# v of the graph convolutions in seven half-block products, its neighbours moved along the LSTM's places

## The chip, the cores and the metric

The kernel runs on one core of a Trainium2 chip. The metric is the device time of one execution in microseconds (us), lower is better; the median of the runs is given. All data are float32. The engines are called PE (TensorE, matrix products), DVE (VectorE), ACT (ScalarE), POOL (GpSimd) and SP (SyncE, which here only issues DMAs).

## The reference

Four residual layers with a layer norm and a relu ahead of each work on x of 128 x 64 x 256 (batch, tokens T, channels D). Layer 0 is a normalised aggregation with a two-layer MLP and batch norms, layers 2 and 3 are attention with one and four heads. The change lies in layer 1:

```python
h = jax.nn.relu(jnp.einsum('ts,bsh->bth', adj, x @ Wg0 + bg0))
h = jax.nn.relu(jnp.einsum('ts,bsh->bth', adj, h @ Wg1 + bg1))
for p in range(1, MAX_SKIP + 1):
    wins = h[:, :nw * p, :].reshape(Bv * nw, p, Hd)
    last = _lstm_last(Wih[p - 1], Whh[p - 1], bih[p - 1], bhh[p - 1], wins)
    h = h.at[:, idx, :].set(last.reshape(Bv, nw, Hd))
```

Two graph convolutions are followed by LSTMs over windows of 1, 2, 3 and 4 tokens, each of which reads what the one before has written to h.

## The kernel before

**Tiles and order.** The batch is cut into 16 chunks of 512 rows (8 batch entries of 64 tokens); two chunks make a superchunk (SUP = 2), so there are 8. The LSTM of layer 1 works on one superchunk at a time: `lstms` (L1443) yields for the windows p = 1 (`single`), 2, 3, 4 (`lstm`, from L1073). While superchunk sc is in its LSTM, the kernel issues between the LSTM's segments the graph convolutions of the chunks of superchunk sc+1, the residual and next layer's norms of the superchunks before, and the first steps (scaling, a reload in another order) of the chunks of sc+2. I call one pass of this loop a round; seven rounds (sc 0 to 6) contain convolutions, and the first of the eight superchunks gets its own ahead of the loop (`first_convolutions`, which the change leaves alone).

The order is written out by hand: PE, DVE, ACT, POOL and SP are under a manual schedule, so that each engine executes in the order in which the program issues. The loop at L1602 counts the segments. Each `yield` of an LSTM makes the next whole number n, a `yield "a"` a half more; these numbers are the *places*, 0 to 21 in a round:

```python
for mark in lstms(sc, hTs[sc]):
    n = n + 0.5 if mark else int(n) + 1
    for u in todo.pop(n, ()):
        next(u)
```

`todo` comes from tables (L1559 to 1570): `CONV[i]` lists for chunk i of a superchunk (0 is called even, 1 odd here) the places at which the steps of `convolutions` are taken, `BEGUN[i]` the places of its first steps, one round ahead; `FIRST` stands for `CONV` in round 0. Window 2 covers places 4 to 7, window 3 places 8 to 13, window 4 places 14 to 21. A place at the end of a window (7, 13) lies between the last cell of one LSTM and the first products of the next.

**The convolution of a chunk** (`convolutions`, L999) has these steps: scaling with layer 0's batch norm (`scaled`, DVE); transposes of 32 x 32 blocks on DVE and a write to DRAM (`put`); its reading back in another order (`get`); `add_squares` onto x (DVE, L298); two halves of layer norm statistics (DVE, L195); two halves of their application (ACT); aggregation over the graph (PE, agg_b, two banks of PSUM); its copies to SBUF (DVE, L1025); `product_v`, v = agg @ Wg0, as 8 PE passes with 512 columns (L934); `bounded` (DVE, L940), which takes the maximum with the negated bias, that is a relu with the bias shifted into a later constant; `product_u`, u = v @ Wg1, 16 PE passes with 256 columns (L948); `biased` (DVE, L954), which adds the constant c2; the second aggregation (agg_c); and two steps of relus to hT (ACT, L959), from which the LSTM reads.

**The LSTM.** Each gate product is made from seven products of half blocks (L1133 for the first step, L1186 for later ones), whose operands' differences POOL or DVE makes (`differences`, L323) and whose parts DVE adds (L1140, L1195) and ACT copies (L1137, L1192). A step ends with a cell on DVE (L1265, L1266), a tanh on ACT (L1267) and the new state on DVE (L1110 to l_hs inside a window; L1112 and L1116 to hT in its last step; k=0 and k=1 are the two halves of the channels). PSUM has four tags with two banks each: x, y, z for the LSTM and ps for the convolutions. Tag x holds product 6 and then product 7 of the same gate in the same half bank; between the two the DVE addition of product 6 has to read it.

Of the kernel before, what the change touches and what calls it, by code (L numbers as in the profile page):

```python
# [8 lines left out]
F32 = mybir.dt.float32  # L9
AF = mybir.ActivationFunctionType  # L10
OP = mybir.AluOpType
AX = mybir.AxisListType

P = 128
# [5 lines left out]
def kernel(  # L20
# [22 lines left out]
    nc = tc.nc  # L43
    B, T, D = x.shape
    H0 = w1t.shape[1]
    KD = D // P
# [653 lines left out]
    with tc.manual_schedule(engines={mybir.EngineType.PE}):  # L700
# [5 lines left out]
        wqkv_sb = stage.tile([P, KD, 3 * D], F32, name="wqkv_sb")  # L706
        wo_sb = stage.tile([P, KD, D], F32, name="wo_sb")
        bg0_sb = stage.tile([P, D], F32, name="bg0_sb")
        bg1_sb = const.tile([P, D], F32, name="bg1_sb")
        wg1_st = stage.tile([P, KD, D], F32, name="wg1_st")  # L710
        nc.sync.dma_start(wqkv_sb, wqkv.rearrange("(k p) f -> p k f", p=P))
        nc.sync.dma_start(wo_sb, wo.rearrange("(k p) f -> p k f", p=P))
        nc.sync.dma_start(bg0_sb, bg0.partition_broadcast(P))
        nc.sync.dma_start(bg1_sb, bg1.partition_broadcast(P))
        nc.sync.dma_start(wg1_st, wg1.rearrange("(k p) f -> p k f", p=P))

        wt = stage.tile([P, 3 * KD, D], F32, name="wt")
# [153 lines left out]
    bias2 = const.tile([P, SKIP, KG], F32, name="bias2")  # L871
    nc.sync.dma_start(bias, bih)
    nc.sync.dma_start(bias2, bhh)

    wih1 = [lasting.tile([P, 3, n, P], F32, tag=f"wih1_{n}", name=f"wih1_{n}") for n in (4, 3)]

# [50 lines left out]
    def by_batch(agg):  # L927
        return agg.rearrange("p k (j e t) -> p e (k j) t", e=2, t=T)
# [12 lines left out]
                                    banks[m].rearrange("p (j n) -> p j n", n=P),  # L941
                                    nc1[:, m, None, :].to_broadcast([P, NJ, P]), OP.max)

    def product_u(c, v):
        banks = [bank(f"u1_{c}_{t}").rearrange("p (j d) -> p j d", d=D) for t in range(NJ // 2)]
        for j in range(NJ):
            for k in range(KD):
                nc.tensor.matmul(banks[j // 2][:, j % 2, :], v[:, k, j * P : (j + 1) * P],  # L948
                                 wg1_sb[:, k, :], start=(k == 0), stop=(k == KD - 1))
        return banks  # L950

    def biased(u, banks):
        for t, ps in enumerate(banks):
# [45 lines left out]
    def convolutions(c):  # L999

        y, h = conv_tile(c)
        for m in range(KD):
            scaled(y, c, m)
        yield
        mid = res.tile([P, Q, CH * KD // Q], F32, tag=f"r{c}", name=f"ym_{c}")
        for k in range(KD):
            nc.vector.transpose(
                mid.rearrange("p b (j k c) -> p k j b c", j=NJ, k=KD)[:, k],
                y[:, k, :].rearrange("p (j b t) -> p j b t", b=Q, t=32))
        far = put(mid, f"y{c}")  # L1010
        yield
        dst = y.rearrange("p k (q n) -> p (k q) n", q=2)
        get(dst, far)
        xs[c] = res.tile([P, NJ, D], F32, tag=f"r{c}", name=f"xs_{c}")
        nc.sync.dma_start(xs[c], xr[c])
        yield
        add_squares(xs[c], xs[c], dst)
        yield
        for stats in norm_halves(xs[c], f"b{c}"):
            yield  # L1020
        yield from apply_halves(h, xs[c], stats, f"b{c}")
        banks = aggregate(h, adjt_bd, f"b{c}")
        yield
        for e, ps in enumerate(banks):
            nc.vector.tensor_copy(by_batch(y)[:, e], ps)  # L1025
        yield
        banks = product_v(c, y)
        yield
        bounded(y, banks)
        yield  # L1030
        banks = product_u(c, y)
        yield
        biased(h, banks)
        yield
        banks = aggregate(h, adjt_bd, f"c{c}")
        yield
        for e, ps in enumerate(banks):
            to_hT(c, e, ps)
            yield
# [518 lines left out]

    EARLY = 0, 3, 5, 7, 9, 9, 13, 15  # L1559
    RESIDUAL = (0, 6, 9), (5.5, 7, 9.5)  # L1560
    CONV = (3, 4, 5, 5.5, 7, 8, 9, 10, 10), (5, 5, 6, 9.5, 11, 11.5, 13, 14, 15, 15.5, 17, 18, 20)
    BEGUN = (11, 11.5, 12, 14.5, 17, 17, 20, 21), (17.5, 19, 19.5, 21)
    RESIDUAL_LAST = (0, 4, 5.5), (3, 5, 9)
    FIRST = (0.5, 0.5, 1, 3, 3, 4, 4, 5, 5.5, 7, 8, 9, 10, 10), (2, 3, 4, 5, 5, 5.5, 6, 9.5, 11, 11.5, 13, 14, 15, 15.5, 17, 18, 20)
    AHEAD = (9, 10), (10, 11)
    LATE = (4.5, 4.5, 5.5, 9, 19.5), (9.5, 9.5, 11, 12, 21)
    LATEST = (4.5, 4.5, 5.5, 9, 9.5), (9.5, 9.5, 10, 11, 11.5)
# [5 lines left out]
    with tc.manual_schedule(engines={mybir.EngineType.PE, mybir.EngineType.DVE, mybir.EngineType.Pool,  # L1573
                                     mybir.EngineType.SP}):
        new_hT(0)
        early = l1.tile([P, 4, KD, CH], F32, tag="gates", name="early", bufs=1)
        convs = {c: (convolutions if c >= SUP else first_convolutions)(c) for c in range(NCH)}
        aheads = {c: ahead(c) for c in range(NCH - SUP)}
        for n, i in enumerate(START):
            if n == 5:  # L1580
                nc.vector.tensor_add(c2, c2_ps[:, :D], bg1_sb)
                nc.vector.tensor_add(bias, bias, bias2)
            for at, fill, name in ((6, 16, "d"), (9, 6, "e"), (10, 6, "f")):
                if n == at:
                    keep_busy(fill, name)
            next(convs[i])
            if n == 1:
                nc.sync.dma_start(wg0_sb, wg0.rearrange("(k p) f -> p k f", p=P))
                nc.sync.dma_start(wg1_sb, wg1.rearrange("(k p) f -> p k f", p=P))
                singles = load_single()  # L1590
                next(singles)
                load_sets(6)
            if n == 9:
                next(singles)
    banks_of("psum1", x=2, y=2, z=2, ps=2)
# [736 lines left out]
```

## Time and profile before

| | |
|---|---|
| median of 2 runs | 1841.06 us (1840.62 and 1841.5) |
| the profiled execution | 1841.82 us |
| its span in the profile | 1839.9 us |
| granted TensorE clock | 0.999 |
| DVE, ACT and POOL busy | 1353.8, 1061.4 and 656.8 us |
| v of a chunk (L934, 8 passes) | 3.43 us on PE |
| u of a chunk (L948, 16 passes) | 3.45 us on PE |
| one round | about 152 us |

Busy time is what an engine's instructions cover; the share of the span is an average over all stages. A timeline line has the start and the duration in us, engine, line and operation, output<-input, shape, and the count of instructions put together; in square brackets the idle time ahead of it and what released it. Matmuls are pipelined, so that durations of neighbouring groups overlap, and what PE really spends is read from start to start.

A round as these places stood in it before (even chunk / odd chunk): agg_b at 3 / 11, its copies at 4 / 11.5, v at 5 / 13, bounded at 5.5 / 14, u at 7 / 15, biased at 8 / 15.5, agg_c at 9 / 17, relus at 10, 10 / 18, 20. For the chunks after these: scaling at 11 / 17.5, put at 11.5 / 19, get at 12 / 19.5, add_squares at 14.5 / 21.

### The profile page before, as it was taken

To read this page: it belongs to the slowest core of one execution; us is meant where nothing else is said; L and a number is where in the kernel's file an instruction comes from. 1 tells how busy PE (TensorE), PEld (TensorE's weight loads), DVE (VectorE), ACT (ScalarE), POOL (GpSimd) and SP (SyncE) were. 2 spreads that over 40 slices of the span, in tenths; PEclk is the share of its full clock that TensorE was granted. 3 is DMA by queue.
4 is the path that set the end of the run, shared out by engine and by line. 5 is a ranking of instruction groups with operands and counts; after the bars stand their busy time and mean duration, and the time that the engine had idled before them with its cause. 6 is when DMAs were issued, how large, how long until landed. Compare 5 with 4: busy or idle time off the path is not lost.

```text
span 1839.9 us, 41662 instructions
## 1 busy us (share of the span) xinstructions
PE 1813.3 (99%) x15847; PEld 1531.8 (83%) x15847; DVE 1353.8 (74%) x3475; ACT 1061.4 (58%) x2538; POOL 656.8 (36%) x916
## 2 busy tenths in 40 slices
PE   8999999999999999999999999999999999999998
PEld 6876866997897899699699789879968887898886
DVE  5768857577667777777777777776676677888897
ACT  5766636557457466655655746566565654455553
POOL 5865823223223321422321332232232215444542
PEclk9999999999999999999999999999999999999999
DMA  3213651233443342253443434225154146544534
GB/s 117 70 58 139 222 218 53 81 115 127 134 143 127 112 153 78 98 146 116 149 149 127 149 115 162 101 93 150 48 172 149 64 110 195 162 139 139 162 108 147
DMA packets 113415, 234.54 MB, mean 127 GB/s; under 512 B 11712, under 2 KB 77120, under 8 KB 113216
## 3 DMA queue, kind: packets, MB, share of 16 engines
q1 hardware_dynamic: 112320, 230.02, 38.5%
q8 instruction: 125, 2.05, 0.5%
q0 software_dynamic: 320, 1.05, 0.2%
q10 hardware_dynamic: 576, 0.82, 0.1%
q14 instruction: 74, 0.61, 0.1%
HBM read 164.21 MB, written 67.63 MB: 126 GB/s over the span
## 4 chain that ended last, share of the span: by engine, by line
PE 89%; DVE 5%; ACT 2%; POOL 2%; issue 1%; DMA 0%; SPq 0%; DVEq 0%; ACTq 0%; POOLq 0%
PE x L1186 23%; PE z L1186 11%; PE y L1186 6%; PE y L1133 4%; PE x L1368 4%; PE y L1368 3%; PE u L948 3%; PE v L934 3%; PE x L1133 3%; PE X L1938 3%; PE X L436 2%; PE X L512 2%; PE v L2062 2%; PE z L1133 2%; PE Y L1938 1%; PE X L1773 1%
## 5 line engine op out<-in xcount | busy, mean ns | idle before, releaser
L1101 ACT ACTIVATE l_gates<-l_gates,bias 128x256 f32<-128x256 f32 (+4 forms) x528 | 238.2, 498 | 210.9 <-DVE l_gates L1195 109.7
L1186 PE MATMUL x<-xd,wset 128*128 128x128 f32 (+2 forms) x1152 | 255.0, 303 | 0.8 <-ACT l_gates L1192 0.8
L1186 PE MATMUL x<-l_hd,wset 128*128 128x128 f32 (+2 forms) x1152 | 254.6, 303 | 0.0
L1252 POOL TENSOR_TENSOR l_gates<-l_gates 128x512 f32<-128x512 f32 (+2 forms) x48 | 75.3, 1570 | 368.0 <-ACT l_gates L1101 368.0
L1195 DVE TENSOR_TENSOR l_gates<-l_gates,x 128x128 f32<-128x128 f32 (+2 forms) x384 | 121.2, 321 | 97.8 <-PE x L1186 95.1
L1186 PEld LDWEIGHTS x<-xd,wset 128*128 128x128 f32 x1152 | 187.7, 191 | 6.4 <-issue 1.4
L1186 PEld LDWEIGHTS x<-l_hd,wset 128*128 128x128 f32 x1152 | 187.8, 191 | 5.0
L1195 DVE TENSOR_TENSOR l_gates<-l_gates,z 128x128 f32<-128x128 f32 (+2 forms) x384 | 102.3, 318 | 105.7 <-PE z L1186 103.7
L1186 PE MATMUL z<-l_hs,wset 128*128 128x128 f32 (+2 forms) x768 | 147.1, 304 | 0.7 <-DVE l_hs L1110 0.7
L1186 PE MATMUL z<-hT,wset 128*128 128x128 f32 (+2 forms) x768 | 146.2, 303 | 0.0
L1192 ACT COPY l_gates<-y 128x128 f32<-128x128 f32 (+2 forms) x192 | 53.2, 290 | 137.7 <-PE y L1186 131.5
L1186 PEld LDWEIGHTS z<-l_hs,wset 128*128 128x128 f32 x768 | 116.8, 191 | 5.8 <-DVE l_hs L1110 2.5
L1186 PEld LDWEIGHTS z<-hT,wset 128*128 128x128 f32 x768 | 117.1, 191 | 3.3
L1101 ACT ACTIVATE l_gates<-x,bias 128x128 f32<-128x128 f32 (+2 forms) x216 | 84.8, 393 | 28.6 <-PE x L1186 25.9
L327 POOL TENSOR_TENSOR xd<-hT 128x128 f32<-128x128 f32 (+2 forms) x72 | 43.2, 600 | 127.5 <-DVE hT L1112 113.8
L1186 PE MATMUL x<-hT,wset 128*128 128x128 f32 (+2 forms) x384 | 85.8, 305 | 0.0
L1186 PE MATMUL x<-l_hs,wset 128*128 128x128 f32 (+2 forms) x384 | 84.9, 303 | 0.0
L1186 PE MATMUL y<-l_hd,wset 128*128 128x128 f32 (+2 forms) x384 | 83.2, 309 | 0.0
L1267 ACT ACTIVATE l_gates<-l_cell 128x256 f32<-128x256 f32 (+2 forms) x144 | 55.3, 384 | 45.8 <-DVE l_cell L1266 45.3
L1186 PE MATMUL y<-xd,wset 128*128 128x128 f32 (+2 forms) x384 | 81.6, 304 | 0.0
L328 POOL TENSOR_TENSOR xd<-hT 128x128 f32<-128x128 f32 (+3 forms) x80 | 51.5, 644 | 67.0 <-DVE hT L1116 29.5
L1110 DVE TENSOR_TENSOR l_hs<-l_gates 128x256 f32<-128x256 f32 (+4 forms) x120 | 51.4, 428 | 29.6 <-ACT l_gates L1159 13.8
(408 smaller groups left out, 4696.8 us busy)
## 6 DMA issues: line engine op xcount, KB each, us to landing
wset<-wfar SPq DMA_DIRECT2D x96, 896.0 KB, 8.4
hT<-far_h SPq DMA_DIRECT2D x124, 128.0 KB, 4.7
far_h<-hm SPq DMA_DIRECT2D x16, 512.0 KB, 3.0
far_n<-xs SPq DMA_DIRECT2D x16, 512.0 KB, 3.4
xs<-far_n SPq DMA_DIRECT2D x64, 128.0 KB, 2.8
far_x<-xs SPq DMA_DIRECT2D x16, 512.0 KB, 3.9
x<-far_x SPq DMA_DIRECT2D x64, 128.0 KB, 3.9
xt<-in_x_dram SPq DMA_DIRECT2D x15, 512.0 KB, 3.9
```

What stands on the lines that cost most here:

```text
L328: lambda: ((third or engine).tensor_tensor(t3, b22, b12, OP.subtract), engine.tensor_tensor(t2, b22, t1, OP.subtract)),
L934: nc.tensor.matmul(banks[m], wg0_sb[:, k, m * P : (m + 1) * P], agg[:, k, :], start=(k == 0), stop=(k == KD - 1))
L948: nc.tensor.matmul(banks[j // 2][:, j % 2, :], v[:, k, j * P : (j + 1) * P], wg1_sb[:, k, :], start=(k == 0), stop=(k == KD - 1))
L1101: nc.scalar.activation(gate(q, c, part), src, AF.Tanh if q == 2 else AF.Sigmoid, bias=bs[:, q * KD + c : q * KD + c + 1])
L1133: nc.tensor.matmul(folded(self.psum(kind)), wsets[p, self.q][:, BLOCKS[kind][0], :], ox[0][kind], start=kind in (1, 5), stop=True, skip_gr ...
L1186: nc.tensor.matmul(folded(self.psum(kind)), wsets[p, self.q][:, BLOCKS[kind][i], :], (ox[self.s] if part == "x" else oh)[kind], start=firs ...
L1192: nc.scalar.copy(gate(self.q, kind // 5, halves[kind // 5]), self.psum(kind))
L1195: nc.vector.tensor_add(gate(self.q, *dst), gate(self.q, *a), self.psum(kind))
L1252: nc.gpsimd.tensor_mul(gates[:, 0, :, :n], gates[:, 0, :, :n], gates[:, 2, :, :n])
L1267: nc.scalar.activation(gate(2, c, part), cells[:, c, part], AF.Tanh)
L1368: nc.tensor.matmul(folded(ps(g, kind)), single_block(KINDS1[kind])[:, g, :], right[kind], start=kind in (2, 5, 1), stop=True, skip_group_c ...
L1938: nc.tensor.matmul(st[c, tag][:, i * CH // 2 : (i + 1) * CH // 2].rearrange("p (a n) -> p a n", n=P), w, operand3(c, kind), start=first an ...
```

## The change

`product_v` and `bounded` remain for the first superchunk. For all later chunks (14) v is computed by a class `SevenV` from seven products of a half block of Wg0 (128 x 128) with a half of the rows (256 columns). POOL makes four differences of the aggregated operand when the copies are issued (the tile is one of three of an existing tag, "g"); four sums of blocks of Wg0 are made once on POOL at the start. The products are issued in four groups, each at a place of its own, with what ACT copies and DVE adds in place in the operand's tile:

- A: products 2, 1 and 5; ACT copies (0,0) and (1,1)
- B: products 6 and 3; ACT copy (0,1), DVE addition (0,0)
- C: DVE addition (0,1); product 7, in the half bank that product 6 used; DVE addition (1,1); the bound for half k=0 and a half of k=1
- D: product 4, and the bound for the rest, straight from PSUM

u is then computed with the order of its token blocks changed, so that its last operands are the last bounded ones. The places after the change (even / odd): agg_b 3 / 12, copies 4 / 12, A 5 / 13, B 7 / 15, C 8 / 15.5, D 8.5 / 16, u 9 / 17, biased 10 / 18, agg_c 11 / 19, relus 11.5, 11.5 / 19.5, 20. For the chunks after these: scaling 12 / 19.5, put 13 / 20, get 14 / 21, add_squares 16 / place 3 of the next round. Also, bg1 is loaded by DMA straight into c2's tile, which saves a constant tile.

```diff
@@ -941,13 +940,76 @@
                                     banks[m].rearrange("p (j n) -> p j n", n=P),
                                     nc1[:, m, None, :].to_broadcast([P, NJ, P]), OP.max)
 
-    def product_u(c, v):
+    def product_u(c, v, swapped=False):
+
         banks = [bank(f"u1_{c}_{t}").rearrange("p (j d) -> p j d", d=D) for t in range(NJ // 2)]
-        for j in range(NJ):
+        for j in (2, 3, 0, 1) if swapped else range(NJ):
             for k in range(KD):
-                nc.tensor.matmul(banks[j // 2][:, j % 2, :], v[:, k, j * P : (j + 1) * P],
+                at = (j + 2) % NJ if swapped and k else j
+                nc.tensor.matmul(banks[j // 2][:, j % 2, :], v[:, k, at * P : (at + 1) * P],
                                  wg1_sb[:, k, :], start=(k == 0), stop=(k == KD - 1))
         return banks
+
+    wg0_sums = w1.tile([P, 4, P], F32, name="wg0_sums")
+
+    def sums_of_wg0():
+        def a(k, m):
+            return wg0_sb[:, k, m * P : (m + 1) * P]
+
+        for d, u, v, op in ((0, a(0, 1), a(1, 1), OP.add), (1, wg0_sums[:, 0], a(0, 0), OP.subtract),
+                            (2, a(0, 0), a(0, 1), OP.subtract), (3, a(1, 0), wg0_sums[:, 1], OP.subtract)):
+            nc.gpsimd.tensor_tensor(wg0_sums[:, d], u, v, op)
+
+    class SevenV:
+
+        def __init__(self, c, y):
+            self.c, self.y = c, y
+            b = {(k, j): y[:, k, halves2[j]] for k in range(KD) for j in range(2)}
+            t = l1r.tile([P, 4, CH // 2], F32, tag="g", name=f"tv_{c}", bufs=3)
+            t = [t[:, i] for i in range(4)]
+            for f in differences(nc.gpsimd, t, b[0, 0], b[0, 1], b[1, 0], b[1, 1]):
+                f()
+            self.at = {1: b[0, 0], 2: b[1, 0], 3: b[1, 1], 4: t[3], 5: t[0], 6: t[1], 7: t[2]}
+            self.to = {(0, 0): b[0, 0], (0, 1): b[0, 1], (1, 0): b[1, 1], (1, 1): b[1, 0]}
+
+        def product(self, kind, ps, first=False):
+            if kind in (1, 2, 4):
+                m, k = {1: (0, 0), 2: (0, 1), 4: (1, 1)}[kind]
+                w = wg0_sb[:, k, m * P : (m + 1) * P]
+            else:
+                w = wg0_sums[:, {5: 0, 6: 1, 7: 2, 3: 3}[kind], :]
+            nc.tensor.matmul(ps, w, self.at[kind], start=first, stop=True, skip_group_check=True)
+
+        def add(self, part, ps):
+            nc.vector.tensor_add(self.to[part], self.to[part], ps)
+
+        def bound(self, m, dst, src):
+            dst, src = [a.rearrange("p (a n) -> p a n", n=P) for a in (dst, src)]
+            nc.vector.tensor_tensor(dst, src, nc1[:, m, None, :].to_broadcast([P, dst.shape[1], P]), OP.max)
+
+        def places(self):
+            xz, w = bank(f"vx_{self.c}"), bank(f"vy_{self.c}")
+            xx, zz, yy = xz[:, : CH // 2], xz[:, CH // 2 :], w[:, : CH // 2]
+            self.product(2, zz, True)
+            self.product(1, xx)
+            nc.scalar.copy(self.to[0, 0], xx)
+            self.product(5, yy, True)
+            nc.scalar.copy(self.to[1, 1], yy)
+            yield
+            self.product(6, xx)
+            nc.scalar.copy(self.to[0, 1], xx)
+            self.add((0, 0), zz)
+            self.product(3, yy)
+            yield
+            self.add((0, 1), yy)
+            self.product(7, xx)
+            self.add((1, 1), xx)
+            self.bound(0, self.y[:, 0], self.y[:, 0])
+            self.bound(1, self.to[1, 1], self.to[1, 1])
+            yield
+            self.product(4, xx)
+            self.bound(1, self.to[1, 0], xx)
+            yield
 
     def biased(u, banks):
         for t, ps in enumerate(banks):
@@ -1023,12 +1085,10 @@
         yield
         for e, ps in enumerate(banks):
             nc.vector.tensor_copy(by_batch(y)[:, e], ps)
-        yield
-        banks = product_v(c, y)
-        yield
-        bounded(y, banks)
-        yield
-        banks = product_u(c, y)
+        v = SevenV(c, y)
+        yield
+        yield from v.places()
+        banks = product_u(c, y, swapped=True)
         yield
         biased(h, banks)
         yield
@@ -1558,10 +1618,12 @@
 
     EARLY = 0, 3, 5, 7, 9, 9, 13, 15
     RESIDUAL = (0, 6, 9), (5.5, 7, 9.5)
-    CONV = (3, 4, 5, 5.5, 7, 8, 9, 10, 10), (5, 5, 6, 9.5, 11, 11.5, 13, 14, 15, 15.5, 17, 18, 20)
-    BEGUN = (11, 11.5, 12, 14.5, 17, 17, 20, 21), (17.5, 19, 19.5, 21)
+    CONV = ((3, 4, 5, 7, 8, 8.5, 9, 10, 11, 11.5, 11.5),
+            (3, 5, 5, 6, 9.5, 12, 12, 13, 15, 15.5, 16, 17, 18, 19, 19.5, 20))
+    BEGUN = (12, 13, 14, 16, 17, 17, 20, 21), (19.5, 20, 21)
     RESIDUAL_LAST = (0, 4, 5.5), (3, 5, 9)
-    FIRST = (0.5, 0.5, 1, 3, 3, 4, 4, 5, 5.5, 7, 8, 9, 10, 10), (2, 3, 4, 5, 5, 5.5, 6, 9.5, 11, 11.5, 13, 14, 15, 15.5, 17, 18, 20)
+    FIRST = ((0.5, 0.5, 1, 3, 3, 4, 4, 5, 7, 8, 8.5, 9, 10, 11, 11.5, 11.5),
+             (2, 3, 4, 5, 5, 5.5, 6, 9.5, 12, 12, 13, 15, 15.5, 16, 17, 18, 19, 19.5, 20))
     AHEAD = (9, 10), (10, 11)
     LATE = (4.5, 4.5, 5.5, 9, 19.5), (9.5, 9.5, 11, 12, 21)
     LATEST = (4.5, 4.5, 5.5, 9, 9.5), (9.5, 9.5, 10, 11, 11.5)
@@ -1578,7 +1640,7 @@
         aheads = {c: ahead(c) for c in range(NCH - SUP)}
         for n, i in enumerate(START):
             if n == 5:
-                nc.vector.tensor_add(c2, c2_ps[:, :D], bg1_sb)
+                nc.vector.tensor_add(c2, c2, c2_ps[:, :D])
                 nc.vector.tensor_add(bias, bias, bias2)
             for at, fill, name in ((6, 16, "d"), (9, 6, "e"), (10, 6, "f")):
                 if n == at:
@@ -1590,6 +1652,7 @@
                 singles = load_single()
                 next(singles)
                 load_sets(6)
+                sums_of_wg0()
             if n == 9:
                 next(singles)
     banks_of("psum1", x=2, y=2, z=2, ps=2)
```

## The prediction

> **What bounds the kernel now.** I read the page first (busy shares, the chain that ended last), then the table of stretches for whole rounds, then the rows of the two lines that compute v and u, then timelines of PE, DVE and ACT around the places that the diff names.
>
> ```profile
> span 1839.9 us, 41662 instructions
> PE 1813.3 (99%) x15847; PEld 1531.8 (83%) x15847; DVE 1353.8 (74%) x3475; ACT 1061.4 (58%) x2538; POOL 656.8 (36%) x916
> ...
> PE 89%; DVE 5%; ACT 2%; POOL 2%; issue 1%; DMA 0%; SPq 0%; DVEq 0%; ACTq 0%; POOLq 0%
> ```
>
> ```profile
> 731.80:883.90 152.10, 152.01 (x1145) 130.39 (x1145) 113.15 (x313) 90.97 (x239) 44.37 (x64) 1.00 0.40 129
> ```
>
> PE sets the end. A round (one superchunk of LSTM with the convolutions of the next between its segments) takes 152.1 us, and PE is idle for 0.1 of it. So work taken off PE pays, but only while the dependent chains of the LSTM stay hidden behind what is left. Those chains are long, and v and u are what hides them:
>
> ```profile
> 787.97 3.62 PE L948 MATMUL u<-wg_sb,cv 128*128 128x256 f32 x16
> 791.43 0.73 PE L1133 MATMUL y<-hT,wset 128*128 128x168 f32 x4
> ...
> 793.14 0.73 PE L1133 MATMUL y<-hT,wset 128*128 128x168 f32 x4
> ...
> 786.45 0.75 DVE L1195 TENSOR_TENSOR l_gates<-l_gates,z 128x256 f32<-128x256 f32 x2 [0.44 <-PE z L1186]
> ...
> 789.29 0.69 DVE L1112 TENSOR_TENSOR hT<-l_gates 128x512 f32<-128x512 f32 x1 [0.69 <-ACT l_gates L1267]
> ...
> 791.71 0.99 DVE L1116 TENSOR_TENSOR hT<-l_gates 128x256 f32<-128x256 f32 x2
> ```
>
> This is place 7, the border of windows 2 and 3. PE's z product lets DVE start the last cell (786.45); the new state is written to hT at 789.98 (k=0, L1112) and 792.70 (k=1, L1116). The next window's first products need it: 791.43 reads k=0, 793.14 reads k=1. Between them PE lives on u, 3.45 us. k=1 is ready 0.44 before its reader: there is hardly any slack. Place 13 (windows 3 to 4) has v in that role, place 15 has u, place 5 has v:
>
> ```profile
> 832.71 3.60 PE L934 MATMUL v<-cv,wg_sb 128*128 128x512 f32 x8
> 836.15 0.61 PE L1133 MATMUL y<-hT,wset 128*128 128x128 f32 x4
> ...
> 837.48 0.61 PE L1133 MATMUL y<-hT,wset 128*128 128x128 f32 x4
> ...
> 842.26 3.62 PE L948 MATMUL u<-wg_sb,cv 128*128 128x256 f32 x16
> 845.71 0.38 PE L1186 MATMUL y<-xd,wset 128*128 128x128 f32 x2
> ...
> 847.50 1.06 PE L1186 MATMUL z<-l_hs,wset 128*128 128x128 f32 x8
> ...
> 836.24 0.33 DVE L1116 TENSOR_TENSOR hT<-l_gates 128x168 f32<-128x168 f32 x1 [0.17 <-ACT l_gates L1267]
> ...
> 845.85 0.43 DVE L1110 TENSOR_TENSOR l_hs<-l_gates 128x256 f32<-128x256 f32 x1 [0.48 <-ACT l_gates L1166]
> ```
>
> **What the Trainium skill says.** "Perfetto Trace Analysis", Optimizing Tensor Performance, asks for independent matmul groups in different PSUM banks, so that evacuation of one overlaps the next; the changed product 7 reuses the bank half of product 6, and must wait for its copy. The same page, Sequencer Loop: an engine instruction waits in its engine's queue for its semaphores. The trace agrees: an in-order engine that waits shows one idle stretch, and all behind it is late. "TensorE: Matmul & The Clock Gate", Back-to-back issue gap, gives 262 cycles for 256 columns and 518 for 512, so halves cost half. Here a 512 pass takes 0.429 us (3.43 over 8) and a 256 pass 0.216 (3.45 over 16): the absolute figures are this float32 kernel's own, the proportion agrees.
>
> **The change part by part.**
>
> *Work removed.* v was 8 passes of 512, 3.43 us. Seven half products of two 256 passes are 7 x 0.432 = 3.02. Saved 0.41 per chunk, 0.82 per round of two chunks, 5.8 us over 14 chunks. This is all there is to gain, beside at most 0.8 us per round of small stalls in before (0.53 of them in 839.27 to 841.36, where DVE's bounded of place 14 delays additions).
>
> *Work added elsewhere.* Per chunk: four POOL subtractions (0.73 each as the like rows of 128x256), three ACT copies (0.37), three DVE additions (0.42); the bound goes from 1.28 to about the same in three pieces. POOL is busy 44 of 152 us and these end long before place 5; ACT 91. The four sums of Wg0 run once in the start, POOL being free; c2's load by DMA and one addition likewise. I take all these at 0; without that cover the POOL part would be 2.9 us per chunk. The added DMA queues nothing in the rounds. The put and get of the next chunk go later on SP (get of the odd chunk to place 21, its reader to place 3 of the next round): a transfer lands in some 4 us, a place lasts 7, so 0; a weight load behind that get is late by at most those 4 us.
>
> *Fill taken away.* v's products now stand as A 1.30 (three), B 0.86 (two), C and D 0.43; u goes one or two places on.
> Place 5: A 1.30 for v 3.43. The z product that reads l_hs stood at s+6.89 (s = start of v, 762.09) and would come at s+4.76; its state (L1110) is ready at s+5.97, trigger 0.05. Stall 1.26; in the first two rounds, without the later layer's norms on DVE ahead of it (ready s+4.69), 0.2.
> Places 7 and 8: with B (0.86) for u the first product comes at a+0.86 (a = 787.97) and waits for k=0 until a+2.05 or so: 1.23 with the changeover. The window's first six products take 1.72, to a+3.8. Then C's product 7 stands in the queue, and waits for B's ACT copy and DVE addition, which sit behind the tail (tanh until a+4.28, L1116 until a+4.73, addition 0.42): a+5.2. Stall 1.43. Together 2.66; without C in the way the k=1 reader alone would give 2.2.
> Place 13: A for v. First products end at E+2.63 (E = 832.71), k=1 is ready at E+3.86. Stall 1.33 with trigger.
> Place 15: B for u. The z product would come 3.55 after the first products' end; its state follows that end by 4.6 to 5.3 (4.92 in before, less the squares that leave place 14.5, plus B's copy and addition). I take 1.5 of 1.1 to 1.9.
>
> *DVE and ACT work put in worse places.* At places 10, 12, 16, 18, 20 the next things on DVE are the additions (L1195) that free the x bank for product 7. Place 10 in before:
>
> ```profile
> 812.25 0.57 DVE L1195 TENSOR_TENSOR l_gates<-l_gates,z 128x168 f32<-128x168 f32 x2 [0.50 <-PE z L1186]
> 812.82 0.33 DVE L1195 TENSOR_TENSOR l_gates<-l_gates,x 128x168 f32<-128x168 f32 x1
> ...
> 813.75 0.45 PE L1186 MATMUL x<-xd,wset 128*128 128x168 f32 x2
> ```
>
> Slack 0.6. The even chunk's biased (1.28) comes between: 0.7. Place 18, odd biased, slack about 0.33: 0.95. Place 20, put's two transposes (1.29): 1.08. Place 16, squares (1.29) and the last bound (0.4), less D's own 0.43 of PE time: 0.95. Place 12: the even chunk's four relus (1.95 on ACT) start at 827.2, so the LSTM's two copies end at 829.7, the additions at 830.3; then the odd chunk's two aggregation copies (1.28), the next chunk's scaling (1.14), and the x addition 0.33 end at 833.05; PE, with the aggregation put at this place (1.35), would be ready at 831.2: 1.88. In before these stood at half places, or with PE work that hid them. The DVE values are certain to 0.1; whether they are paid depends on how far DVE runs ahead: 0 to 5.6 for the five together; I take all, since DVE's queue is in order.
>
> *Sum per round:* 1.26 + 2.66 + 0.7 + 1.88 + 1.33 + 1.5 + 0.95 + 0.95 + 1.08 = 12.3; less 0.82 and 0.8: 10.7 for rounds three to six. First two: 9.6. The seventh has no next chunks (no scaling at 12, squares at 16, transposes at 20): 7.5. 2 x 9.6 + 4 x 10.7 + 7.5 = 69.5. The profiled execution took 1841.8 (span 1839.9): 1911. The median, 1841.06, is 0.8 less, so it makes no difference.
>
> **Rivals.**
> A, only the fill counts: the DVE work of places 10 to 20 is absorbed. Then places 5, 7 and 8, 13, 15 stay, 6.75, less 1.6 is 5.1 per round; with product 7 not in the way and place 15 at its low end 4.3. Some 30 to 34 us, less in the first rounds: 1869 to 1876. For: DVE is 74% busy, with room. Against: order, not room, decides.
> B, not slower: the border chains end with PE. What ends them are DVE's L1116 and L1110 behind tails whose start PE sets; if those tails, freed of the squares and of bounded beside them, ended 2.1 us earlier at each of places 5, 7, 13, 15, there would be no stall, and 1841.8 less 5.8 (with before's stalls gone as well, 11) is 1831 to 1836. Point of decision: L1116 done by a+2.6 at place 7. Against: between 786.45 and 792.70 DVE has only this chain's own operations; nothing there is removed.
> C, they compound: a late chain delays the next step's states as well, so that stalls of places 10 and 12, 16 to 20 are paid again in the z products behind. Half as much again: 105, so 1945.
> The products not being seven is no rival: the program has them.
>
> **How the numbers follow.** Main case 0.60, own range 1885 to 1935; A 0.20; B 0.08; C 0.12. The range holds A and the main case: 1862 to 1938. Slower by over 2% (above 1877.9; 2% is about what a measurement of this kernel can tell from no change) is the main case and C, 0.72; A and B give 0.27 within; 0.01 is left for faster.
>
> **What would show it.** PE's busy time falls by about 5.8 while the rounds grow to about 162. PE waits for L1112's and L1116's successors at the borders of windows, 1.2 and 1.4 us each in all seven rounds; waits for the z products by l_hs at places 5 and 15; x products waiting for DVE additions behind biased, squares and transposes. Rounds of 156 to 157 with border waits alone are A; rounds of 151 are B; rounds above 166 are C. The sum is wrong if the DVE tail at place 7 ends before a+4, or if the x products at 10, 16, 18, 20 start without wait.

## The result, and the profile after

The changed kernel takes 1922.73 us (median of 2 runs, 1922.35 to 1923.12) against 1841.06: a ratio of 1.044, 95% interval 1.0423 to 1.0458, slower by 81.7 us. The forecast was 1911 in a range of 1862 to 1938, with 0.72 for slower. The interval is 0.2% to each side, much finer than the 2% that the prediction took for what a measurement of this kernel can tell.

The first lines of the page of the changed kernel, and the shares of its last chain:

```profile
span 1921.2 us, 42020 instructions
...
PE 1837.2 (96%) x15931; PEld 1549.5 (81%) x15931; DVE 1374.7 (72%) x3531; ACT 1067.6 (56%) x2580; POOL 704.2 (37%) x976
...
PE 74%; DVE 13%; ACT 6%; POOL 3%; issue 3%; DMA 0%; ACTq 0%; DVEq 0%; POOLq 0%
```

The chain that ends last now runs for 13% of the span on DVE and 6% on ACT (5% and 2% before). One round, from A of the even chunk to the next, in the table of stretches (length, then PE busy):

```profile
798.12:962.48 164.36, 155.63 (x1158) 133.05 (x1157) 115.71 (x322) 92.21 (x244) 50.93 (x72) 1.00 0.35 119
```

PE was idle for 0.1 us of a round; now it is for 8.7, at a full granted clock. PE's waits by what ended them (us in total, times, longest), the whole program:

```profile
PE x L1246 <- DVE l_gates L1255: 17.2, 26, 1.0
PE y L1193 <- DVE hT L1172: 9.7, 15, 1.0
PE z L1246 <- DVE l_hs L1170: 4.7, 6, 0.8
PE y L1193 <- DVE l_gates L1200: 4.7, 6, 0.8
PE vx L981 <- DVE cv L984: 4.5, 7, 0.9
PE y L1193 <- POOL xd L328: 4.4, 8, 0.6
PE y L1193 <- ACT l_gates L1197: 3.8, 8, 0.5
PE agg_b L228 <- ACT hT L1021: 3.3, 7, 0.5
PE x L1246 <- ACT l_gates L1252: 3.2, 10, 0.4
```

(In the changed kernel L981 is v's product, L984 and L988 its addition and bound on DVE, L995, L997 and L1000 its copies on ACT, L1016 biased, L1021 the relus, L949 u, L1087 the aggregation's copies; the LSTM's L1110, L1112, L1116, L1133, L1137, L1140, L1186, L1192 and L1195 have become L1170, L1172, L1176, L1193, L1197, L1200, L1246, L1252 and L1255. In the experiments that edit the program these numbers lie a few lines further on.) The first row is the x products behind DVE work, the second the borders of windows, the third the new state inside window 2 (place 5), the fifth product 7. The last three are waits for ACT that the forecast did not have.

Place 7 of that round in the timelines of PE, ACT, DVE and POOL:

```profile
823.67 0.59 PE L981 MATMUL vy<-cv,wg_sums 128*128 128x256 f32 x2
825.31 0.84 PE L1193 MATMUL y<-hT,wset 128*128 128x168 f32 x4 [1.04 <-DVE hT L1172]
...
828.36 0.70 PE L981 MATMUL vx<-tv,wg_sums 128*128 128x256 f32 x2 [0.61 <-DVE cv L984]
828.89 0.73 PE L1193 MATMUL y<-hT,wset 128*128 128x168 f32 x4
...
831.32 0.81 PE L1193 MATMUL y<-xd,wset 128*128 128x168 f32 x4 [0.56 <-POOL xd L328]
...
827.42 0.35 ACT L1000 COPY cv<-vx 128x256 f32<-128x256 f32 x1
...
827.89 0.41 DVE L984 TENSOR_TENSOR cv<-cv,vx 128x256 f32<-128x256 f32 x1
```

B starts at a = 823.24. The first product waits for k=0 until a+2.07 (forecast a+2.05); product 7 waits for the copy and addition behind the tail until a+5.12 (forecast a+5.2). The third wait, for POOL, was not forecast.

I took every LSTM product of the round in both traces and compared the starts. Less the fill that was put in or taken out, these stalls were added (us, for rounds three to six):

| where | forecast | measured |
|---|---|---|
| place 5 | 1.26 | 1.38 |
| places 7 and 8 | 2.66 | 3.43 |
| place 10, biased | 0.7 | 0.65 |
| place 12, relus, copies, scaling | 1.88 | 2.18 |
| place 13 | 1.33 | 1.68 |
| place 15 | 1.5 | 0.93 |
| place 16, squares and bound | 0.95 | 0.91 |
| place 18, biased | 0.95 | 0.90 |
| place 20, relus and transposes | 1.08 | 0.97 |
| first products of window 2, squares at 3 | 0 | 1.01 |
| small stalls of before, gone | -0.8 | -0.95 |
| work | -0.82 | -0.82 |
| round | 10.7 | 12.27 |

Counted from one even chunk's v to the next, the first two rounds came out 11.6 longer (forecast 9.6) and the next four 12.2 on average. What follows the seventh's v is 8.5 longer (7.5), and the first v comes 0.9 later: 2 x 11.6 + 4 x 12.2 + 8.5 + 0.9 = 81.4, and the two spans differ by 81.3.

At place 20 the transposes are the smaller part. The x products wait 0.60 for ACT's copy, which stands behind the odd chunk's relus, and then 0.37 for DVE's addition behind the transposes:

```profile
926.12 1.03 ACT L1021 ACTIVATE hT<-agg_c 128x256 f32<-128x256 f32 x2
926.95 0.47 ACT L1252 COPY l_gates<-x 128x128 f32<-128x128 f32 x2
...
927.31 0.49 PE L1246 MATMUL x<-xd,wset 128*128 128x128 f32 x2 [0.34 <-ACT l_gates L1252]
```

### The profile page after: what moved, and what is told of

Read it like the earlier page. It is cut to its first block, busy times and chain, and to the rows that moved or that the text cites. A ratio compares the mean times of both kernels' runs of the same rounds, so it can differ in the third digit from the quotient of the medians.

```text
span 1921.2 us, 42020 instructions
## 1 busy us (share of the span) xinstructions
PE 1837.2 (96%) x15931; PEld 1549.5 (81%) x15931; DVE 1374.7 (72%) x3531; ACT 1067.6 (56%) x2580; POOL 704.2 (37%) x976
## 4 chain that ended last, share of the span: by engine, by line
PE 74%; DVE 13%; ACT 6%; POOL 3%; issue 3%; DMA 0%; ACTq 0%; DVEq 0%; POOLq 0%
PE x L1246 18%; PE z L1246 9%; PE y L1246 4%; PE x L1428 4%; PE y L1193 3%; PE y L1428 3%; PE u L949 3%; PE X L2001 2%; PE X L436 2%; ACT l_gates L1161 2%; PE X L512 2%; PE v L2125 2%; DVE l_gates L1255 2%; PE x L1193 1%; DVE l_gates L1200 1%
## 5 line engine op out<-in xcount | busy, mean ns | idle before, releaser
L1246 PE MATMUL x<-xd,wset 128*128 128x128 f32 (+2 forms) x1152 | 259.7, 307 | 21.0 <-DVE l_gates L1255 17.2
L1246 PE MATMUL x<-l_hd,wset 128*128 128x128 f32 (+2 forms) x1152 | 254.5, 303 | 0.0
L1246 PEld LDWEIGHTS x<-xd,wset 128*128 128x128 f32 x1152 | 187.3, 191 | 35.9 <-DVE l_gates L1255 24.8
L1255 DVE TENSOR_TENSOR l_gates<-l_gates,x 128x128 f32<-128x128 f32 (+2 forms) x384 | 117.8, 320 | 121.8 <-PE x L1246 119.6
L1246 PEld LDWEIGHTS x<-l_hd,wset 128*128 128x128 f32 x1152 | 187.8, 191 | 5.0
L1255 DVE TENSOR_TENSOR l_gates<-l_gates,z 128x128 f32<-128x128 f32 (+2 forms) x384 | 102.6, 318 | 119.7 <-PE z L1246 116.8
L1246 PE MATMUL z<-l_hs,wset 128*128 128x128 f32 (+2 forms) x768 | 147.6, 305 | 5.4 <-DVE l_hs L1170 4.7
L1246 PE MATMUL z<-hT,wset 128*128 128x128 f32 (+2 forms) x768 | 146.2, 303 | 0.0
L1252 ACT COPY l_gates<-y 128x128 f32<-128x128 f32 (+2 forms) x192 | 54.5, 292 | 150.9 <-PE y L1246 148.6
L1246 PEld LDWEIGHTS z<-l_hs,wset 128*128 128x128 f32 x768 | 116.5, 191 | 12.3 <-DVE l_hs L1170 9.2
L1246 PEld LDWEIGHTS z<-hT,wset 128*128 128x128 f32 x768 | 118.0, 191 | 4.0
L327 POOL TENSOR_TENSOR xd<-hT 128x128 f32<-128x128 f32 (+2 forms) x72 | 48.5, 674 | 110.5 <-DVE hT L1172 86.1
L1246 PE MATMUL x<-hT,wset 128*128 128x128 f32 (+2 forms) x384 | 85.1, 303 | 0.0
L1246 PE MATMUL x<-l_hs,wset 128*128 128x128 f32 (+2 forms) x384 | 84.8, 303 | 0.0
L1246 PE MATMUL y<-l_hd,wset 128*128 128x128 f32 (+2 forms) x384 | 83.9, 310 | 0.3
L1246 PE MATMUL y<-xd,wset 128*128 128x128 f32 (+2 forms) x384 | 81.4, 304 | 0.6
L1327 ACT ACTIVATE l_gates<-l_cell 128x256 f32<-128x256 f32 (+2 forms) x144 | 55.3, 384 | 47.7 <-DVE l_cell L1326 47.2
L1170 DVE TENSOR_TENSOR l_hs<-l_gates 128x256 f32<-128x256 f32 (+4 forms) x120 | 51.4, 428 | 29.8 <-ACT l_gates L1226 13.8
```

Of the source, the lines that this page charges most:

```text
L327: return [lambda: engine.tensor_tensor(t1, b12, b11, OP.subtract), lambda: ((third or engine).tensor_tensor(t3, b22, b12, OP.subtract), en ...
L1170: nc.vector.tensor_mul(hn[:, c, part], gate(3, c, part), gate(2, c, part))
L1246: nc.tensor.matmul(folded(self.psum(kind)), wsets[p, self.q][:, BLOCKS[kind][i], :], (ox[self.s] if part == "x" else oh)[kind], start=firs ...
L1252: nc.scalar.copy(gate(self.q, kind // 5, halves[kind // 5]), self.psum(kind))
L1255: nc.vector.tensor_add(gate(self.q, *dst), gate(self.q, *a), self.psum(kind))
L1327: nc.scalar.activation(gate(2, c, part), cells[:, c, part], AF.Tanh)
```

## The experiments

All were timed beside the kernel before, whose median was 1841.6 in each set.

**Whole v at the new places.** The changed kernel with

```diff
-        yield from v.places()
-        banks = product_u(c, y, swapped=True)
+        banks = product_v(c, y)
+        yield
+        yield
+        bounded(y, banks)
+        yield
+        yield
+        banks = product_u(c, y)
```

> The changed kernel's places with v whole again (8 passes of 512 at places 5 and 13, bounded in one step at places 8 and 15.5). Theory (the places cost, not the seven products): places 5 and 13 lose their stalls of 1.4 and 1.7 us, places 7 and 15 have no fill at all, the waits of product 7 and behind C go; per round about 1.8 us less than the changed kernel, 162.6 us, so 1905 to 1914 us in all. Rival (the seven-product form costs: its additions on DVE, copies on ACT, waits of product 7): with v whole the time returns to 1845 to 1855 us.

1916.79 us, ratio 1.0408 (1.0393 to 1.0424). So 75 of the 82 us are there without any seven products: the new order of the work costs them. At these places the seven products cost 6 us more than v whole, not 5.8 less. The stalls are not the same ones, since v whole fills places 5 and 13 and leaves 7 and 15 without any fill. It came out 3 us above the expected span of times. PE is idle for 1.9 us at place 7, and in five of the seven rounds the passes behind that run at half speed (see the last section), which takes about 8.5 us (estimate: five stretches of 3.41 us at half clock).

```profile
822.95 1.21 PE L1197 MATMUL y<-hT,wset 128*128 128x168 f32 x4 [1.91 <-DVE hT L1176]
```

**Biased half a place earlier**, 9.5 and 17.5 in `CONV`:

> The changed kernel with one edit: biased at places 9.5 and 17.5 in place of 10 and 18. Theory (DVE's order decides: biased stands ahead of the x additions at 10 and 18): 0.65 + 0.9 us less per round, 10.9 us over seven rounds, 1910 to 1914 us. Rival (DVE's work is absorbed, and those x products wait for something else): 1920 to 1923 us.

1916.32 us (1.0406; 1.039 to 1.0421): 6.4 less than the changed kernel, where 10.9 were expected. The odd chunk gave its 0.90 per round, 7 x 0.9 = 6.3. At place 10 the stall of 0.65 went and one of 0.71 appeared 2.3 us later, at the second group of x products:

```profile
850.10 0.51 DVE L1326 TENSOR_TENSOR l_cell<-l_cell,l_gates 128x336 f32<-128x336 f32 x1 [1.50 <-POOL l_gates L1312]
850.52 0.56 DVE L1255 TENSOR_TENSOR l_gates<-l_gates,x 128x168 f32<-128x168 f32 x2
...
850.90 0.55 PE L1246 MATMUL x<-xd,wset 128*128 128x168 f32 x2 [0.43 <-DVE l_gates L1255]
```

DVE's cell waits for POOL's product of gates, and the x additions stand behind the cell. The stall was moved and not removed.

**Only the rest.** v and u whole, at 5, 13, 7, 15 as in the kernel before; everything else at the changed kernel's places:

> The converse of the run with u back: v whole at 5 and 13, bounded at 5.5 and 14, u whole at 7 and 15, as in the kernel before; only the steps behind u and those of the next chunks stand at the changed kernel's places (biased 10 and 18, second aggregation 11 and 19, relus 11.5 and 19.5, the odd chunk's first aggregation and copies 12, scaling 12, put 13 and 20, squares 16 and 3). Theory (DVE's and ACT's order at these places costs on its own, whatever fills the borders): the stalls counted in the changed kernel at places 10, 12, 16, 18, 20 and 3, 0.65 + 2.2 + 0.9 + 0.9 + 1.0 + 0.9 = 6.5 us per round, come back: 1878 to 1888 us. Rival (only the lost fill counts): 1842 to 1850 us.

1899.58 us (1.0314; 1.0299 to 1.033), 58 more than before. The DVE and ACT steps cost by themselves, at the places named: 0.65 at 10, 1.8 at 12, 0.9 at 16 and 18, 1.0 at 20, 1.0 in window 2. It is more than the 6.5 per round expected (8.8), since this order has stalls of its own: 1.1 at place 9, which the second aggregation leaves without fill (the second row), 0.55 in window 4's first products, 0.84 between 16 and 18.

```profile
PE x L1248 <- DVE l_gates L1257: 18.5, 33, 0.6
PE y L1248 <- ACT l_gates L1163: 7.0, 7, 1.0
```

**Only v and u.** The changed kernel's groups and u at their places, but biased at 9.5 and 17.5, second aggregation 10 and 18, relus 11 and 19, next chunks' scaling 11 and 19, put 11.5 and 19, squares 14.5 and 21. The odd chunk's first aggregation and its copies stay at 12:

> The changed kernel with v's groups and u at its places (5, 7, 8, 8.5, 9 and 13, 15, 15.5, 16, 17), but the DVE and ACT steps moved off the places ahead of the x additions: biased 9.5 and 17.5, second aggregation 10 and 18, relus 11 and 19, 20; next chunks' scaling 11 and 19, put 11.5 and 19, squares 14.5 and 21. The odd chunk's first aggregation and copies stay at 12. Theory: of the 6.5 us per round of these places some 5 go (biased at 9.5 gave back nothing of its 0.65 in the run with it alone): 1887 to 1897 us. Rival (they only hide behind the border stalls): 1912 to 1922 us.

1902.81 us (1.0332; 1.0315 to 1.0349), 20 less than the changed kernel, and 61 above before. Per round 2.7 us were given back: the stalls of 10, 12, 16, 18 and window 2 are gone (5.5), but the relus at 11 make a new wait of 1.8 (an x product for the ACT copy behind them), and place 15 waits 0.6 longer. The stall of 20 is gone too, and one of the same size, 1.0, stands at 19, where this order has a relu, the scaling and the transposes. The border stalls at 5, 7 and 8, and 13 are the same as in the changed kernel:

```profile
PE y L1193 <- DVE hT L1172: 10.0, 15, 1.0
```

So each half alone costs about 60. They do not add to 120 in the changed kernel because each test order has stalls of its own: 2.5 us per round in the one, 2.4 in the other, and the 1.0 at 19 or 20 is counted in both. Over seven rounds that is about 41 us (estimate), against 38 to be explained.

**u back, A and B together.** A and B at 5 and 13, C and D at 5.5, 6 and 14, 14.5, u at 7 and 15, the rest as in the changed kernel; and the same groups with the rest at the places of before:

> The changed kernel's v in seven products, with A and B at places 5 and 13, C at 5.5 and 14, D at 6 and 14.5, and u back at 7 and 15; all DVE and ACT steps behind u and all steps of the next chunks stay at the changed kernel's places. Theory: the stalls of places 7 and 8 (3.4 us) and 15 (0.9) go, those of 5 and 13 shrink from 3.1 to about 1.1, and 0.5 gained at place 9 is lost: 5.9 us less per round, near 158.5, and 1880 to 1886 us. If the places of DVE's work were everything, 1910 or more; if the fill were everything, 1842 to 1850.

> v in seven products at places as near as can be to those before: A and B at 5 and 13, C at 5.5 and 14, D at 6 and 14.5, u at 7 and 15, everything else at the places of the kernel before. Theory: work is 0.82 us per round less, stalls of about 0.5 us each at places 5 and 13 remain (A and B are 2.16 us where v was 3.43): within 4 us of the kernel before, 1837 to 1845 us. Rival (the seven-product form itself costs by its extra DVE and ACT work): 1860 us or more.

1964.47 us (1.0669; 1.0653 to 1.0685) and 1919.05 us (1.042; 1.0402 to 1.0437). Both expectations failed by some 80 us, and the second rival, that the form itself costs, seemed right. The trace of the second, PE and ACT at place 5:

```profile
793.17 0.59 PE L981 MATMUL vy<-tv,wg_sums 128*128 128x256 f32 x2
797.96 1.19 PE L981 MATMUL vx<-tv,wg_sums 128*128 128x256 f32 x2 [4.19 <-ACT cv L995]
798.94 1.06 PE L981 MATMUL vy<-cv,wg_sums 128*128 128x256 f32 x2
...
796.92 0.63 ACT L1226 ACTIVATE l_gates<-l_cell 128x512 f32<-128x512 f32 x1 [1.65 <-DVE l_cell L1225]
797.46 0.35 ACT L995 COPY cv<-vx 128x256 f32<-128x256 f32 x1
```

Product 6 adds onto product 1 in the same half bank, so ACT must copy it first. That copy takes 0.35 us, but it is queued behind the LSTM's tanh, which waits for DVE's cell. There are 43.9 us of such waits in 14 chunks, and some 27 us more are lost in passes at half clock behind them (estimate: a granted clock of 0.985 against 0.999, over 1917 us). Nothing like it is in the changed kernel, where a place lies between A and B. Splitting v brings hops from PE to ACT or DVE and back to PE, and a hop at a border waits for the LSTM's whole tail.

**One group to a place, as early as may be.** A 5, B 5.5, C 6, D and u 7 (odd: 13, 14, 14.5, 15), the rest as before:

> Seven products, one group to a place, but as early as the kernel before had v: A 5, B 5.5, C 6, D 7 with u at 7; odd chunk A 13, B 14, C 14.5, D 15 with u at 15; everything else as in the kernel before. Theory: product 6 no longer stands behind ACT's tail (44 us of waits in the run with A and B together go), u hides the borders at 7 and 15, A alone leaves 1.4 us at place 5 and 1.7 at 13, C's DVE work at place 6 costs up to 1.7: about 4 us per round more than before, 1862 to 1876 us. Rival (the form costs wherever it stands): 1900 us or more.

1920.68 us (1.0431; 1.0415 to 1.0446), 45 above the expected span of times. Product 6's wait is gone; now u waits for the bound of product 4, which is behind the tail on DVE. PE at place 7:

```profile
824.93 0.59 PE L981 MATMUL vx<-tv,wg_sb 128*128 128x256 f32 x2
825.37 1.89 PE L949 MATMUL u<-wg_sb,cv 128*128 128x256 f32 x8
830.05 3.56 PE L949 MATMUL u<-wg_sb,cv 128*128 128x256 f32 x8 [2.79 <-DVE cv L988]
...
829.58 0.42 DVE L988 TENSOR_TENSOR cv<-vx,nc 128x256 f32<-128x256 f32 x1
```

All in all 32.2 us in 14 chunks, before the slow passes that follow (8 in 3.40 us, where they take 1.73). So with D at 7, u cannot hide that border.

**C behind, together with D** (8.5):

> The changed kernel with C of the even chunk at place 8.5, together with D, in place of 8. Theory: product 7 no longer waits in front of the reader of the new state at place 8 (0.9 us less), but that reader then waits for the state itself until 4.8 us after the last cell's product, and D waits for DVE's addition behind product 7: within 3 us of the changed kernel, 1920 to 1926 us. Rival (product 7's place is the whole cost at places 7 and 8): 0.9 + 0.8 us less per round, 1909 to 1913 us.

1948.7 us (1.0585; 1.0569 to 1.0602), 26 above the changed kernel. At 8 the stalls went as the rival had it in part (0.3 before the reader of k=1 and the 0.79 for POOL); but D waits up to 3.0 us for DVE's addition behind product 7 (20.9 us, 7 times). It is a hop inside one place again, and again the expectation left out what is queued ahead of it: DVE comes to this addition only after the next step's cell and state.

**Fewer hops.** Product 4 into the unused half bank and into A, one more copy and addition, the bound in one step in C. A stands at 5, B at 5.5, C at 6, u at 7 (odd: 13, 14, 14.5, 15), the rest as before:

```diff
             nc.scalar.copy(self.to[1, 1], yy)
+            self.product(4, ww)
             yield
...
+            nc.scalar.copy(self.to[1, 0], ww)
             yield
...
-            yield
-            self.product(4, xx)
-            self.bound(1, self.to[1, 0], xx)
+            self.add((1, 0), xx)
...
```

> Seven products in three groups in place of four: product 4 gets a half bank of its own and goes into A (four products, 1.73 us), its sum is made by one more ACT copy and DVE addition; the bound is made in one step in C. So u no longer waits for a bound that follows a product at its own place. A 5, B 5.5, C 6, u 7; odd A 13, B 14, C 14.5, u 15; everything else as in the kernel before. Theory (what hurt the run with one group to a place was the bound behind the tail at 7 and 15, 4.6 and 4.3 us per round; what is left is A's short fill): places 5 and 13 keep about 1.1 and 1.3 us, place 6 up to 0.5, less 0.8 of work: about 2 us per round, 1850 to 1860 us. Rival (the extra DVE and ACT work of the form costs): 1890 us or more.

1943.37 us (1.0556; 1.0541 to 1.057), 83 above the expected span of times. Product 4 got a wait for ACT's copy from the other half of its bank (47.7 us, 14 times, the longest 4.4), and at 15 u still waits for the bound (18.5 us, 7 times). The even chunk's u at 7 does not wait any more.

**The even chunk alone**, in these three groups, with v whole for the odd one and everything else at the places of before; once with the norms moved from 4.5 to 8.5, once not. In these two the even chunk's u takes its halves in the order of the first superchunk's, so its values are others; its passes are the same.

> The three-group form for the even chunk only, v whole for the odd one as in the kernel before, and the later layer's norms of the even chunk moved from place 4.5 to 8.5 (their application to 9), off the chain that ends at place 5. Theory: at place 5 the z product comes 5.2 us after v's start and its state is ready after 4.7, so A's 1.73 us hide it; u hides 7, whole v hides 13, u hides 15. Work is 0.41 us per round less: 1837 to 1841 us, at or a little under the kernel before. If norms at 8.5 or C at place 6 cost: 1845 to 1852 us.

> The same with the norms left at place 4.5. Theory: the z product at place 5 waits from 5.2 to 6.0 us after v's start in the five rounds that have these norms, with the restart 1.1 us: 1842 to 1846 us, 4 to 6 us above the run with the norms moved. Rival (place 5's stall has nothing to do with DVE's queue): the same time as that run.

1912.81 us (1.038; 1.0366 to 1.0394) and 1889.41 us (1.026; 1.0246 to 1.0274). Both have product 4's wait; with the norms at 4.5:

```profile
PE vy L981 <- ACT cv L998: 28.0, 7, 4.4
```

Moving the norms shortens the wait from 4.4 to 3.1 us, but at 8.5 they cost 3.9 in window 3's first step, with passes at half clock behind it. The order of the two is the opposite of the expected one: norms are no free good at 8.5.

**Product 4 first.** The even chunk alone, with the norms at 4.5, and product 4 issued ahead of ACT's copy:

```diff
-            nc.scalar.copy(self.to[1, 1], yy)
             self.product(4, ww)
+            nc.scalar.copy(self.to[1, 1], yy)
```

> As the run with the even chunk alone and the norms at 4.5, with one line moved: product 4 is issued ahead of the ACT copy from the other half of its bank, so that the program gives it no wait for that copy. Theory (the 4.4 us before product 4 at place 5 in that run are this wait behind ACT's tail, with the half-clock passes after it): they go; left are the z product's wait for the state at place 5 (1.1 us with the restart, in the five rounds with norms at 4.5) and 0.6 at place 6, less 0.41 of work: 1844 to 1852 us. Rival (the copy is not what product 4 waits for, or the form costs elsewhere as much): 1875 us or more.

1849.88 us (1.0043; 1.0029 to 1.0057), as expected: 40 us by one line's order (the even chunk's u takes its halves as in the changed kernel again, with the same passes). The 28.0 us of waits are gone, and the granted clock is 0.999 in place of 0.989. What is left per round are stalls of 0.84 at place 5 and 0.5 at 6, each with 0.1 more in the passes behind it, against 0.41 of work saved. PE's waits in it:

```profile
PE z L1253 <- DVE l_hs L1177: 4.1, 6, 0.7
PE x L1253 <- DVE l_gates L1262: 3.8, 7, 1.7
```

So in one of two chunks the seven products can be had for 8 us, where no hop meets a border and u keeps its place; but no version that I ran beats the kernel before. This form for both chunks was not run.

## Why the prediction was right, point by point

**What bounds.** That v and u are the fill for the borders, and that the chains there end on DVE at fixed times after PE's last product, was right: the state's deadline at place 7, a+2.05, was met to 0.02 us. That the order of places is what costs is shown by the runs with v whole (75 of 82 us), with the rest alone (58) and with v and u alone (61).

**The terms of the sum.** Seven of nine stalls agree within 0.4 us, but not all for the reasons given. Places 7 and 8 were 0.77 too small: the wait for POOL's operands (0.79) was missed. Place 13 was 0.35 too small: the reader of k=1 starts 0.4 after its state is written, since it also waits for ACT's copy from the y bank (L1197), which is queued behind A's two copies. The extra copies were taken at 0. At place 12, 0.9 of the 2.18 is the aggregation's wait for the relus on ACT, which the sum did not have. At place 20 the size was right partly by luck: the relus make the larger part. Place 15 was 0.57 too large: the state came 4.3 us after the window's first products, under the range of 4.6 to 5.3, because B's copy and addition came behind it on ACT and DVE. The first passes after a wait start about 0.1 late each time; the sum had this only in part.

**"So 0" for the next chunk's steps** was the step that failed. I followed the odd chunk's reload to place 3 of the next round and priced the DMAs, not the two DVE additions themselves, which stand there ahead of window 2's additions, and there took 2.36 us in place of 1.29: 1.0 per round. With 1.29 next to nothing would have been left of that stall (estimate: 1.01 less 1.07). The slower pace could be read in the trace of before, where the odd chunk's additions at place 21 take 2.52 us beside POOL and delay nothing.

**The small stalls of before.** The 0.53 in window 4's first products did not go, though bounded left place 14: other waits took their place. 0.54 was gained in the y and z products behind place 9, which u now covers, and 0.36 in window 1.

**What would show it.** PE's busy time was to fall by 5.8. It rose by 23.9. A pass is counted busy beyond the start of the next, so that passes ahead of a gap cover more of the time; the saving cannot be read from it. The count of passes tells: 15931 - 15847 = 84 = 14 x (14 - 8), and A lasts from 798.12 to 799.41, 1.29 where 1.30 was priced.

**Rivals.** A (fill only) falls by the run with only the rest moved: 58 us, so DVE's work was not absorbed. B falls by the waits at all borders. C, compounding, is not seen: behind the stalls of places 10, 12, 16, 18 and 20 no z product has a wait that it did not have before.

**The saving, 5.8 us.** It was priced rightly as passes, and in the time it cannot be seen: the run with v whole at the same places is 6 us faster than the changed kernel. What I missed in the experiments, and not in the prediction, is how dear a hop is where ACT or DVE has the LSTM's tail ahead of it; most expectations that failed, failed by that.

## What to carry to other kernels

A large product that waits for nothing is worth more than its passes: splitting it into parts that need copies between them takes away the fill that it gave, and in this kernel every hop from PE to another engine and back cost what was queued on that engine, not the 0.35 us of the copy. Before work is moved in an in-order schedule, write beside each place what the next engine's queue must do first, for DVE and ACT steps as for PE's.

## What the runs showed of the hardware

**The clock after a gap.** In the run with A and B together at place 5, four stretches around the gap (length, PE, PEld, DVE, ACT, POOL busy, granted clock, DMA):

```profile
790.00:793.00 3.00, 3.00 (x16) 2.66 (x15) 1.59 (x4) 2.59 (x5) 0.95 (x2) 1.00 0.00 0
793.00:797.90 4.90, 0.76 (x4) 0.33 (x2) 4.01 (x12) 3.25 (x9) 1.42 (x2) 0.82 0.00 0
797.90:803.10 5.20, 5.14 (x12) 4.13 (x13) 3.98 (x13) 0.93 (x3) 1.55 (x5) 0.51 0.00 0
803.10:810.00 6.90, 6.90 (x33) 6.08 (x32) 1.52 (x5) 1.49 (x4) 0.91 (x3) 1.00 0.01 1
```

After 4.2 us without work PE runs 5.2 us at a clock of 0.51: a pass of 256 columns takes 0.43 us, not 0.216, so that some 2.5 us are lost on top of the gap (5.2 x 0.49). A gap of 2.8 us did the same in the run with u behind D (8 passes in 3.40 us), and so did the 1.9 us at place 7 in the run with whole v, but there in five rounds of seven only. Two stretches of that run, behind a gap with half clock and around a gap without (497.31):

```profile
823.27:826.68 3.41, 3.41 (x14) 3.41 (x13) 3.23 (x7) 2.48 (x10) 1.35 (x3) 0.50 0.98 393
490.00:500.00 10.00, 7.65 (x38) 6.15 (x36) 6.53 (x15) 4.73 (x13) 0.59 (x1) 1.00 0.93 309
```

In the clock records of these traces the half clock behind a gap lasts 3.41 us or, less often, 6.83, and its starts in one trace lie a whole number of times 3.41 us apart. If a grid of 3.41 us is laid through them, the five gaps with half clock lie whole in one cell, and the other two are cut by a border, with 1.7 us at most on one side. In C behind together with D, two of the seven gaps of 2.98 us had no half clock; both are cut, into 1.8 and 1.2 us. So what counted was an idle time of about 1.9 us or more within one cell of 3.41. Single gaps of up to 1.67 us in the rounds had no half clock behind them in any run: 1.04 in the changed kernel, 1.55 with only v and u moved, 1.62 in one group to a place, 1.67 with product 4 first. The Trainium skill, "TensorE: Matmul & The Clock Gate", What's actually happening, says that PE goes to half clock after an idle window of about 3.4 us, free-running, and needs as long to come back. The length and the free-running window agree with 3.41 us here; but a window that was idle for 1.9 us of it was enough, so the measurement decides.

**DVE beside POOL.** The squares at place 3 of the changed kernel, with POOL's differences beside them:

```profile
952.76 2.36 DVE L298 TENSOR_TENSOR xs<-xs,cv 128x512 f32<-128x512 f32 x2
...
952.24 1.18 POOL L329 TENSOR_TENSOR xd<-hT,xd 128x256 f32<-128x256 f32 x1
953.50 1.06 POOL L330 TENSOR_TENSOR xd<-hT,xd 128x256 f32<-128x256 f32 x1
954.53 1.18 POOL L327 TENSOR_TENSOR xd<-hT 128x256 f32<-128x256 f32 x1
```

Alone the pair of squares takes 1.29 us and a difference 0.73. In the kernel before, the pair at place 21 took 2.52 us beside POOL's differences:

```profile
736.31 2.52 DVE L298 TENSOR_TENSOR xs<-xs,cv 128x512 f32<-128x512 f32 x2
...
736.56 1.73 POOL L329 TENSOR_TENSOR xd<-hT,xd 128x512 f32<-128x512 f32 x1
```

Both read two operands from SBUF; biased, which reads u from PSUM, ran beside POOL at 1.28 in before. The skill's "SBUF — State Buffer", Who interferes with whom, says that a DVE instruction with two SBUF inputs contends with a POOL one that reads SBUF, and one with a single SBUF input, outside some faster modes, does not: this agrees. It is also behind the 0.56 us for POOL at place 8: there POOL's differences took 0.99 and 0.71 where they take 0.54, beside the bound in C (1.51, where it takes 1.02 in the run with A and B together), and the wait went with C moved away.
